# One kernel, one planned order: the delays the planner assumes between engines are changed

## The chip, the core and the metric

The kernel runs on one core of one Trainium2 chip. The metric is the device time of one execution in microseconds (us). Before the change it is 1154.88 us, the median of three runs (1153.9 to 1155.04).

A core has five engines with a queue each, and every queue runs strictly in its own program order: TensorE (PE, matmuls; its weight loads are shown as PEld), VectorE (DVE), ScalarE (ACT), GpSimd (POOL) and SyncE (SP, which here only issues DMAs). Between queues there are semaphores: an instruction that waits holds up everything behind it on its own engine.

## What is computed

One transformer block on 2 x 2048 tokens of width 512: causal attention with 16 query heads of 32 and a single shared key/value head, a layernorm, a mixture of 8 experts (top 2, hidden width 128), a second layernorm.

```python
qkv = einsum('bsd,ed->bse', x, Wqkv_w) + Wqkv_b            # q: 16 heads of 32, one k, one v
scores = where(causal, einsum('bqhd,bkd->bhqk', q, k) / sqrt(32), min)
ctx = einsum('bhqk,bkd->bqhd', softmax(scores), v)
x = layernorm(x + einsum('bsd,ed->bse', ctx, out_w) + out_b)
top, sel = top_k(x @ router_w.T, 2);  gate = softmax(top)
h = silu(xb @ w1[e]) * (xb @ w3[e]);  y = sum over sel of gate * (h @ w2[e])     # bf16
x = layernorm(x + y)
```

## The kernel before

**Tiles and blocks.** The 4096 tokens are 32 tiles T of 128, in 8 groups G of 4. In its batch entry a tile has `own = T % 16` earlier tiles, so it is weighed against `own + 1` key tiles. That makes 272 blocks (tile, key tile) in all, 16 of them in the last tile, T = 31.

**One block.** PE makes the scores of all 16 heads (`three<-qT,kT_g` and one bank, 8 row-tiled matmuls of 64 x 512; lines 1081 to 1095). ACT takes the exponential in two instructions, 1536 elements from `three` and 512 from the bank, into a tile `pT` (for the tile's own diagonal block: `acc`, which POOL then masks). PE weighs the values (`cs<-pT,v_g`, lines 1161 to 1166). DVE adds `pT` to `acc` (`add_up`, line 1204), so that the sums of the softmax need one pass at the end. There is only one `three`, three `pT`, two `acc` and four more PSUM banks (`bank`) that everything else shares.

**Behind the last block of a tile** (`after`): sums by PE with a matrix of ones, a 32 x 32 transposition on DVE (`lT`), reciprocals, `ctxT`, the output projection (`bank<-woT,ctxT`), the residual, then `layernorm`: DVE statistics (`st`, `mv`, `r`), two small POOL instructions on `r`, and ACT or, in the last tile, DVE for `x`.

**Experts** (`experts`, by groups of four tiles; singly in the last group): transposition of x1, the router (`gates`), then for each tile and each half of the experts `up` (w1), `half` (w3), ACT's tanh into `a`, a DVE product, a POOL product with the gates (`a<-a,gt`; in single tiles the gate is applied on DVE instead), a DVE product into `h`, a DMA transposition of `h`, and `down` with the second residual and layernorm.

**What sets the order.** A planner written in the kernel, class `Order` (lines 67 to 236), runs at build time. Every piece of work is a generator that yields `step(engine, us, ...)`: the engine, an assumed duration, the buffers it needs (`acquire`), the marks it needs (`after`), a priority and, for filler work, a due time. The planner keeps a clock for every engine, takes the engine whose next step can start first, of its ready steps the one of lowest `prio`, and emits its instructions there. Each engine's queue is then kept in just this order (`keep_in_program_order`, line 252: all instructions carry L248 in the profile). Scores of attention have `prio` 0, weighings 1, and fillers (projections, output projections, experts) 1.5 or more unless their due time is near, when they go to -0.5.

A step of `us` occupies its engine for `us`. What depends on it can start only `LAT[engine]` later:

```python
self.now, self.end = t, t + us
if s.eng != SP:
    self.busy[s.eng] = self.end
self.end += self.LAT[s.eng]
```

`mark` and `free` record this later time, so LAT is the delay that the planner assumes for a semaphore between engines. On PE a change of the array's tiling costs `TURN` besides. The durations that bear on the change are: scores 0.86 on PE, the exponential 0.25 + 0.44 per bank on ACT (1.57 for `three`), 2.3 on DVE for an addition to `acc`, 2.25 on POOL for `a<-a,gt` and for the mask, 1.95 on POOL for both `r` instructions. Nothing of LAT reaches the chip: there the semaphores decide, and only the order is fixed.

The whole program is also built a second time behind a check of the sums (`run(True)`); that part isn't executed with these inputs.

Of the kernel before, what the change touches and what calls it, by code (L numbers as in the profile page):

```python
# [33 lines left out]
PE, ACT, DVE, POOL, SP = "PE", "ACT", "DVE", "POOL", "SP"  # L34
# [32 lines left out]
class Order:  # L67
# [1 line left out]

    LAT = {PE: 0.3, ACT: 0.15, DVE: 0.15, POOL: 0.15, SP: 0.0}
    LOOK = {DVE: 1.0}
    TURN = {FULL: 0.1, ROW: 0.2, COL: 0.115, TILE: 0.115}
    CAP = 5.0
# [1 line left out]
    def __init__(self, banks, **rings):  # L77
        self.rings = {name: [n, []] for name, n in rings.items()}
        self.banks = [None] * banks
        self.busy = {e: 0.0 for e in self.LAT}  # L80
        self.sig = {}
# [11 lines left out]
    def advance(self, gen, got):  # L93
        end = self.end
        try:
            s = gen.send(got)
        except StopIteration:
            return
        lat = s.lat if s.lat is not None else -self.LAT[PE] if s.open_ else 0.0
        self.count += 1  # L100
# [119 lines left out]
    def issue(self, t, p):  # L220
# [8 lines left out]
# [3 lines that stand above are left out]
        if s.due is not None and s.eng == PE:  # L232
# [1080 lines left out]
```

## Time and profile before

| | us |
|---|---|
| median of the three runs | 1154.88 |
| the profiled execution, device time | 1154.49 |
| its span, first to last instruction | 1152.7 |
| PE busy | 1087.3 (94%) |
| DVE busy | 923.6 (80%) |
| ACT busy | 735.8 (64%) |
| POOL busy | 452.2 (39%) |

The granted TensorE clock was 0.998 over the run. Busy time of matmuls has modelled ends, so PE's 94% says that PE is seldom without work, not that it is at its peak. Each group of instructions has its mean duration: an addition to `acc` on DVE takes 2349 ns, x238; an exponential of `three` 1543 ns; of a bank 682 ns; `a<-a,gt` on POOL 2060 ns, x56; the two `r` instructions on POOL 1572 and 1350 ns. After the first 30 us the DMA engines are busy for 6 to 20% of any longer stretch.

### The profile page before, as it was taken

The numbers are of one execution on the slowest core, as the hardware profiler recorded it, in microseconds if no ns is written. First come the engines' busy times: TensorE is split into PE (matmuls) and PEld (weight loads), VectorE is DVE, ScalarE is ACT, GpSimd is POOL, SyncE is SP. The second block draws the span as 40 slices with busy tenths as digits, with TensorE's granted clock in tenths as the row PEclk, the third lists the DMA queues.
The fourth block names the chain that finished last, engine by engine and source line by source line (L and its number), as shares of the span: only waits on it lengthen the run. The fifth ranks groups of instructions, "written<-read, shape, count | busy, mean of one in ns | idle before, by whom it ended". The sixth has DMA issues, their size and how long they took to land.

```text
span 1152.7 us, 29615 instructions
## 1 busy us (share of the span) xinstructions
PE 1087.3 (94%) x13046; PEld 329.4 (29%) x13046; DVE 923.6 (80%) x1171; ACT 735.8 (64%) x839; POOL 452.2 (39%) x291
## 2 busy tenths in 40 slices
PE   8999999999999999999999999999999899899975
PEld 4322222222322233232222222223233233233222
DVE  2348767878998789989747877779989999999975
ACT  2455667576676677775656556666676667767561
POOL 3212432213451245445325324416556455345110
PEclk9999999999999999999999999999999999999999
DMA  9301001002110021111001000001011011011011
GB/s 253 75 17 56 10 10 48 11 11 56 30 47 1 11 66 29 38 30 38 19 20 56 20 10 19 20 20 38 20 37 40 20 26 42 19 30 48 20 29 31
DMA packets 57404, 40.94 MB, mean 36 GB/s; under 512 B 42729, under 2 KB 43753, under 8 KB 57266
## 3 DMA queue, kind: packets, MB, share of 16 engines
q1 hardware_dynamic: 47248, 34.63, 11.2%
q0 software_dynamic: 9360, 3.15, 2.4%
q8 instruction: 104, 1.70, 0.6%
q10 hardware_dynamic: 658, 1.18, 0.3%
q14 instruction: 34, 0.28, 0.1%
HBM read 25.58 MB, written 8.39 MB: 29 GB/s over the span
## 4 chain that ended last, share of the span: by engine, by line
PE 58%; DVE 28%; issue 5%; POOL 4%; ACT 4%; DMA 0%; DVEq 0%; ACTq 0%; POOLq 0%
PE bank L248 33%; DVE acc L248 15%; PE three L248 14%; PE cs L248 11%; ACT pT L248 2%; POOL r L248 2%; POOL a L248 2%; DVE st L248 2%; DVE x L248 2%; DVE h L248 2%; DVE lT L248 1%; DVE ctxT L248 1%; DVE a L248 1%; DVE fine L248 1%; DVE mx L248 1%
## 5 line engine op out<-in xcount | busy, mean ns | idle before, releaser
L248 DVE TENSOR_TENSOR acc<-acc,pT 128x2048 f32<-128x2048 f32 x238 | 559.1, 2349 | 36.7 <-PE cs L248 22.0
L248 ACT ACTIVATE pT<-three,bias 128x1536 f32<-128x1536 f32 x240 | 370.3, 1543 | 266.9 <-PE bank L248 211.2
L248 PE MATMUL three<-qT,kT_g 32*64 32x512 f32 x3264 | 299.5, 612 | 29.9 <-ACT pT L248 21.4
L248 PE MATMUL bank<-qT,kT_g 32*64 32x512 f32 (+1 forms) x1216 | 304.8, 590 | 0.2 <-ACT qT L248 0.2
L248 PE MATMUL cs<-pT,v_g 128*32 128x512 f32 x1920 | 255.4, 603 | 1.6 <-ACT c_sb L248 0.9
L248 POOL TENSOR_TENSOR r<-r,neg_half 128x1 f32<-128x1 f32 x64 | 100.6, 1572 | 360.1 <-DVE r L248 348.4
L248 POOL TENSOR_TENSOR a<-a,gt 128x512 f32<-128x512 f32 x56 | 115.1, 2060 | 164.2 <-DVE a L248 164.2
L248 ACT ACTIVATE pT<-bank,bias 128x512 f32<-128x512 f32 x240 | 163.6, 682 | 0.0
L248 PE MATMUL bank<-w_sb,x1b 128*32 128x512 bf16 x2048 | 127.3, 380 | 2.5 <-DVE x1b L248 0.7
L248 POOL TENSOR_SCALAR_AFFINE_SELECT acc<-acc 128x2048 f32<-128x2048 f32 x32 | 72.2, 2256 | 140.6 <-ACT acc L248 140.6
L248 PE MATMUL bank<-woT,ctxT 128*32 128x512 f32 x1024 | 119.7, 594 | 3.9 <-DVE ctxT L248 3.6
L248 PE MATMUL bank<-xT,wqT 128*32 128x512 f32 x1024 | 122.4, 594 | 0.0
L248 PEld LDWEIGHTS three<-qT,kT_g 32*64 32x64 f32 x3264 | 60.4, 129 | 194.7 <-ACT pT L248 138.5
L248 PEld LDWEIGHTS cs<-pT,v_g 128*32 128x32 f32 x1920 | 40.6, 108 | 178.0 <-issue 172.7
L248 POOL TENSOR_SCALAR r<-mv,r 128x1 f32<-128x1 f32 x62 | 83.7, 1350 | 6.1
L248 PEld LDWEIGHTS <-x1b 128*32 128x32 bf16 x2048 | 57.5, 97 | 84.4 <-issue 47.5
L248 ACT ACTIVATE acc<-three,bias 128x1536 f32<-128x1536 f32 x32 | 49.4, 1544 | 38.0 <-PE three L248 23.0
L248 PE MATMUL bank<-w_sb,hT 128*32 128x512 bf16 x1024 | 62.4, 379 | 2.5 <-DVE h L248 1.4
L248 ACT ACTIVATE x<-x,r 128x512 f32<-128x512 f32 x62 | 50.5, 818 | 6.5 <-POOL r L248 6.5
L248 PEld LDWEIGHTS bank<-woT,ctxT 128*32 128x32 f32 x1024 | 31.1, 109 | 79.9 <-issue 64.3
L248 DVE STREAM_TRANSPOSE lT<-bank 128x512 f32<-128x512 f32 x32 | 22.9, 715 | 38.4 <-PE bank L248 38.4
L248 DVE TENSOR_TENSOR x<-bank,xr 128x512 f32<-128x512 f32 x32 | 22.0, 688 | 39.1 <-PE bank L248 33.3
(110 smaller groups left out, 962.3 us busy)
## 6 DMA issues: line engine op xcount, KB each, us to landing
xg<-in_L_attn_x_dram SPq DMA_DIRECT2D x32, 256.0 KB, 4.0
xr<-in_L_attn_x_dram SPq DMA_DIRECT2D x32, 256.0 KB, 2.6
out_dram<-x SPq DMA_DIRECT2D x32, 256.0 KB, 2.0
w_sb<-in_L_ffn_w_dram POOLq DMA_DIRECT2D x8, 256.0 KB, 9.1
wq_n<-in_L_attn_Wqkv_w_dram ACTq DMA_DIRECT2D x4, 256.0 KB, 5.9
wo_n<-in_L_attn_out_w_dram SPq DMA_DIRECT2D x1, 1024.0 KB
w_sb<-in_L_ffn_w_dram POOLq DMA_DIRECT2D x1, 1024.0 KB, 15.7
hT<-h SPq DMA_TRANSPOSE x31, 3.1
```

The source lines that it names most:

```text
L248: return lambda *a, **k: self.issue(getattr(self.engine, name)(*a, **k))
```

## The change

Two of five delays in the planner become shorter, one becomes longer:

```diff
-    LAT = {PE: 0.3, ACT: 0.15, DVE: 0.15, POOL: 0.15, SP: 0.0}
+    LAT = {PE: 0.18, ACT: 0.1, DVE: 0.15, POOL: 1.0, SP: 0.0}
```

No instruction's work changes. The listing of both programs' queues shows the same matmuls, exponentials, additions and DMAs, in another order on every engine:

- PE changes the tiling of its array 686 times before and 685 times after; all 272 blocks use `three` and one bank in both.
- Between one block's scores and the next block's, PE gets other work. Before, most often a weighing and two filler steps; after, most often a weighing and one.
- The `up` steps of the groups 0 to 6 begin behind score block 47, 80, 116, 162, 194, 217 and 241 before, and behind 61, 109, 134, 192, 215, 242 and 263 after. Group 6 is in work during blocks 241 to 253 before; after, it falls into the last tile (blocks 257 to 272), with its x1 transposed behind block 258.
- In the last microseconds, before: `down` of tile 30, transposition of `h` of tile 31, `down` of tile 31. After: transposition of `h` of tile 31, `down` of tile 30, `down` of tile 31. The router's `trscT` of tile 30 stands before the output projection of tile 31 in the old order and behind it in the new. On DVE the second half of `h` of tile 30 moves in between the halves of tile 31.

## The prediction

> **What bounds the kernel now.** First the page: engines, then the chain that ended last.
>
> ```profile
> PE 1087.3 (94%) x13046; PEld 329.4 (29%) x13046; DVE 923.6 (80%) x1171; ACT 735.8 (64%) x839; POOL 452.2 (39%) x291
> ...
> PE 58%; DVE 28%; issue 5%; POOL 4%; ACT 4%; DMA 0%; DVEq 0%; ACTq 0%; POOLq 0%
> ```
>
> PE sets the end with DVE's help. Where, the stretches say (us; busy of PE, PEld, DVE, ACT, POOL):
>
> ```profile
> 562.00:623.00 61.00, 60.39 (x612) 17.82 (x596) 32.58 (x49) 33.20 (x41) 21.27 (x18) 1.00 0.10 31
> ...
> 949.00:998.00 49.00, 45.58 (x590) 13.98 (x585) 46.46 (x68) 36.40 (x42) 20.23 (x17) 1.00 0.14 39
> ...
> 1112.00:1153.00 41.00, 25.32 (x315) 10.54 (x315) 24.51 (x75) 10.07 (x17) 3.27 (x6) 0.93 0.10 29
> ```
>
> Early PE is full and DVE half idle; late in a batch entry both are at 93 to 95%; the last 41 us are a chain that fills neither. Third, PE's timeline, one block with two filler steps and two blocks without:
>
> ```profile
> 304.78 0.67 PE L248 MATMUL three<-qT,kT_g 32*64 32x512 f32 x6
> ...
> 305.82 1.06 PE L248 MATMUL cs<-pT,v_g 128*32 128x512 f32 x8
> 306.70 1.91 PE L248 MATMUL bank<-w_sb,hT 128*32 128x512 bf16 x32
> 308.54 0.67 PE L248 MATMUL three<-qT,kT_g 32*64 32x512 f32 x6
> ...
> 344.16 0.68 PE L248 MATMUL three<-qT,kT_g 32*64 32x512 f32 x6 [0.61 <-ACT pT L248]
> ...
> 346.94 0.68 PE L248 MATMUL three<-qT,kT_g 32*64 32x512 f32 x6 [0.67 <-ACT pT L248]
> ...
> 348.13 1.54 ACT L248 ACTIVATE pT<-three,bias 128x1536 f32<-128x1536 f32 x1 [0.67 <-PE bank L248]
> ```
>
> From start to start, scores take 1.04 us, a weighing 0.88, two fillers 1.84: 3.76. With no filler the single `three` sets 2.78: 1.19 until ACT starts (346.94 to 348.13), 1.54 of exponential, 0.05 back to PE. Last, POOL:
>
> ```profile
> 1000.17 2.28 DVE L248 TENSOR_TENSOR acc<-acc,pT 128x2048 f32<-128x2048 f32 x1
> ...
> 1000.33 3.01 POOL L248 TENSOR_TENSOR a<-a,gt 128x512 f32<-128x512 f32 x1 [15.64 <-DVE a L248]
> ...
> 1003.38 0.69 DVE L248 TENSOR_TENSOR h<-bank,a 128x512 bf16<-128x512 f32 x1 [0.93 <-POOL a L248]
> ```
>
> The tile `a` (ns, least, median, most), and the list of waits:
>
> ```profile
> L248 POOL TENSOR_TENSOR a<-a,gt x56: 1029/2954/3157, 243.5 to 1042.7; 128x512 f32<-128x512 f32 x56
> ```
>
> ```profile
> DVE h L248 <- POOL a L248: 16.9, 23, 1.2
> ```
>
> POOL's product takes 2.95 us (median) beside an addition, 1.03 at best, and DVE then stands before `h`: 16.9 us in 23 waits.
>
> **The new delays against the chip.** The old plan thinks the bare loop lasts 0.86 + 0.2 (turn) + 0.3 + 1.57 + 0.15 = 3.08 us; the new, 0.86 + 0.2 + 0.18 + 1.57 + 0.1 = 2.91; the trace has 2.78. Scores, weighing and one filler (0.98 with the turn) make 2.90, so one filler leaves the old plan a hole, into which it starts a second; the new plan stops at one. Gaps of 2.75 to 3 us between scores, by these step prices, grow from 22 to 111 of 271, those of 3.5 to 4 fall from 140 to 38. For POOL the old plan has 2.25 + 0.15 = 2.4 for `a`, the new 3.25 (trace 2.95); for both `r` 2.1 and 2.95 (trace 1.57 + 1.35 = 2.92).
>
> **PE's work: nothing.** I price each PE step by the lower-quartile start-to-start time of its kind and count both listings: 1062.1 us before, 1062.6 after; 686 and 685 turns. The change can only move lost time, 1152.7 - 1062.1 = 90.6: 11.9 until tile 1's first score (at 42.6; priced 30.8), 49.8 until tile 31's (1054.8), 10.1 until the last score (1111.9), 18.7 behind it.
>
> **Until tile 31.** I cut the way to tile 31 into 15 stages, at tiles 1, 4, 7, 9, 11, 13, 15, 17, 20, 22, 24, 26, 28, 29, 30 and 31, and price PE's and DVE's work in each (DVE's by the means of its rows, a tile beginning with its first addition). Before: tiles 9 to 11 PE 78, DVE 75, took 79; 13 to 15 PE 96, DVE 101, took 102; 29 to 30 PE 44, DVE 47, took 50. The larger of the two, stage by stage, is 47, 76, 64, 78, 85, 101, 61, 53, 45, 63, 74, 82, 49, 47, 54, in sum 979; the stretch took 1012, 3.4% more. After: 49, 74, 54, 76, 82, 96, 66, 55, 42, 67, 65, 80, 50, 42, 58, in sum 956: the expert work left for tile 31. 956 x 1.034 = 988.5, from 42.0: tile 31's first score at 1030.5, where before had 1054.8.
>
> **What moves and costs nothing.** ACT's instructions move too; ACT is 64% busy and needs 1.54 + 0.69 of each 2.90, and what it delays is in the 3.4%. The mask on POOL (2.02 median) is now planned at 3.25; in both orders 31 of 32 tiles' own weighings stand over 6 us of PE work behind their scores, against 1.19 + 1.54 + 0.69 + 2.02 = 5.4 needed: other blocks' work covers it. On SP, group 6's stores and `h` transpositions move into the last tile past the `xr` loads (2.0, 3.1 and 2.6 us to land): `xr` is wanted 10 us later, and DMA is 10% busy there; without that cover a store costs 2 us once.
>
> **POOL.** The DVE work queued between `a` and its `h` is POOL's cover. Before, 11 of 56 lie at 2.3 and 19 below 2.8; after 8 below 2.8, most at 3 to 5.7. What is missing to 3.2 sums to 20.9 before (measured wait 16.9) and 17.8 after; but six of the new ones are nearly uncovered (0 to 1.4), where no addition runs beside POOL: at 1.3 each instead of 3.2, 6.5 remains. A saving of 3 to 10; I take 5, as some waits lie where PE is the longer. 1025.5. If no wait is on the path, 0.
> The GPSIMD Engine Reference of the Trainium skill (Specifications) says that GpSimd shares its SBUF interfaces with VectorE and contends with two-input VectorE instructions. By that POOL's cost is a stretch, no constant delay, and the 1.0 is wrong wherever DVE isn't adding; by the rule the saving nears 10, by a constant 2.95 it is 3.
>
> **Tile 31 until `lT`.** Before, its own block is weighed 11.2 us behind its first score; after, PE has 13.9 in between, + 0.9 lost as before: 1040.3. From there to the DVE transposition `lT` the old trace takes 53.2 (1066.1 to 1119.28) for 48.1 of priced DVE work, of which the bare `three` loop costs some 3.4 more than in the new order; without it 49.8, a factor of 1.035. New: DVE 68.5, PE 63.4. 68.5 x 1.035 = 70.9: `lT` at 1111.2. Bounds 68.5 and 68.5 x 1.106 = 75.8.
>
> **From `lT`.** Before 33.4 us. `lT` to the end of the output projection: + 0.4, as DVE's `x1b` is on the way. Then the router of tile 30 starts behind the projection: by the durations in the trace the two halves of `h` of tile 31 end 15.4 us behind the projection where before it was 13.4, and tile 30's second half at 13.6. `down` of tile 30 stands ahead of tile 31's in PE's queue and needs a DMA transposition (3.1 us to landing, median): it starts at some 17.1, tile 31's at 19.0, before 14.7. + 4.3. Queued behind that are the residual, layernorm and the last store, the end itself. Bounds: + 2 (the 13.4 to 15.4 alone) and + 6 (landing 1.7 later). 33.4 + 0.4 + 4.3 = 38.1.
>
> **Sum.** 1111.2 + 38.1 = 1149.3 of span. The median stands 2.2 above the profiled span (1154.88 - 1152.7): **1151.5 us**, 0.3% faster. Startup: its four transpositions change places, + 0 to 0.5, hidden by the first loads.
>
> **Rivals.** *The last tile eats more than the rest gains* (slower). Place: tile 31 between its own weighing and `lT`. Group 6's eight halves and four layernorms now run there, each a chain PE, ACT, DVE, POOL, DVE through two `a`; the old last 41 us show what chains do (DVE 24.5 of 41). If the stretch takes 82 instead of 70.9 (factor 1.2 on DVE): 1162.6. It decides from 76.6 on, where the total passes 1157.2. Against: 14 additions are there to fill DVE. *No change*: POOL's waits lie where PE is longer, nothing is saved: 1156.5, and with a stage factor of 1.033 1155.5. *Much faster*: with honest delays the stages lose 2% (tiles 9 to 11 lost 1.4, 1 to 4 2.6): 956 x 1.02, 13.4 less: 1138.1. For it: ACT and POOL are modelled closely now; against: in a 2.90 rhythm DVE (2.35 of it an addition) has no slack for `a` and `h`. That the order stays the same is excluded by the listing.
>
> **How the numbers follow.** Forecast (own range 1144 to 1152.5) 0.37, much faster 0.12, no change 0.16, slower 0.35. What can be told from no change is 0.2%, 2.3 us: faster 0.49, same 0.16, slower 0.35. Range: the stage factor between 1.026 and 1.042 is 8 us either way; POOL 3.5 or 5; `lT` + 5; tail + 2: 1139 to 1167.
>
> **What would show it.** Right: first score of tile 31 about 25 to 30 us earlier than 1054.8; DVE's wait for POOL `a` below 12; PE's last `down` behind a DMA transposition; from `lT` to the end about 38. Wrong: more PE waits for ACT or DVE in the 2.9 rhythm (a stage factor above 1.04), or `lT` more than 76 behind the own weighing.

## The result and the profile after

| | before | after |
|---|---|---|
| median of the runs on one chip, us | 1154.45 (4 runs) | 1168.94 (4 runs, 1167.58 to 1172.56) |
| ratio, 95% interval | | 1.013 [1.0105, 1.0155] |
| profiled execution, us | 1154.49 | 1172.56 |
| its span, us | 1152.7 | 1170.7 |
| first score of tile 31 at | 1054.8 | 1035.5 |
| last score at | 1111.9 | 1124.3 |
| from the last score to the end | 40.8 | 46.4 |

The change makes the kernel 1.3% slower. The profiled execution is the slowest of the four; its sums are made against its own 1170.7 us. The page of the changed kernel, engines and the chain that ended last:

```profile
PE 1095.9 (94%) x13046; PEld 330.9 (28%) x13046; DVE 928.8 (79%) x1171; ACT 736.8 (63%) x839; POOL 432.5 (37%) x291
...
PE 62%; DVE 25%; issue 6%; ACT 5%; DMA 1%; POOL 1%; DVEq 0%; ACTq 0%; POOLq 0%; SPq 0%
```

The shares hardly move, so the page alone does not say where 18 us went. The stretches do (us; busy time of PE, PEld, DVE, ACT, POOL; granted clock, DMA share, GB/s): tiles 1 to 30, the start of tile 31, two stretches of its blocks, and what is behind the last score.

```profile
42.00:1035.00 993.00, 951.34 (x11326) 271.50 (x11329) 814.29 (x913) 669.24 (x747) 377.01 (x234) 1.00 0.10 28
1035.00:1052.00 17.00, 15.94 (x225) 6.31 (x221) 13.14 (x19) 11.01 (x15) 10.86 (x11) 1.00 0.13 33
1052.00:1080.00 28.00, 23.83 (x288) 6.33 (x280) 24.96 (x44) 15.85 (x18) 11.49 (x7) 0.94 0.10 30
1080.00:1124.00 44.00, 38.80 (x567) 16.54 (x562) 35.96 (x65) 21.20 (x28) 20.46 (x15) 1.00 0.15 38
1124.00:1170.70 46.70, 29.77 (x395) 14.14 (x387) 28.90 (x102) 11.62 (x20) 3.57 (x8) 0.92 0.18 48
```

Until tile 31 PE is busy for 96% of the time. In tile 31 it is 85% at 1052 to 1080, where DVE is at 89%. In the old order PE was at 84% behind tile 31's own weighing as well (38.49 of the 46 us from 1066 to 1112), but without group 6's work; the change brings that work here, and it does not fill PE. What happens in it is on PE's timeline (two transpositions of group 6's x1, the own block's weighing, a later weighing, then scores of three blocks):

```profile
1040.94 0.66 PE L248 MATMUL bank<-ident,x 128*128 128x128 f32 x4 [0.86 <-DVE h L248]
1041.80 0.66 PE L248 MATMUL bank<-ident,x 128*128 128x128 f32 x4 [0.20 <-ACT pT L248]
...
1050.68 1.07 PE L248 MATMUL cs<-acc,v_g 128*32 128x512 f32 x8
...
1060.17 1.63 PE L248 MATMUL cs<-pT,v_g 128*32 128x512 f32 x8 [0.72 <-ACT pT L248]
1061.73 0.67 PE L248 MATMUL three<-qT,kT_g 32*64 32x512 f32 x6
...
1064.57 0.68 PE L248 MATMUL three<-qT,kT_g 32*64 32x512 f32 x6 [1.73 <-ACT pT L248]
...
1073.73 0.85 PE L248 MATMUL three<-qT,kT_g 32*64 32x512 f32 x6 [1.72 <-ACT pT L248]
...
1074.31 1.13 PE L248 MATMUL three<-qT,kT_g 32*64 32x512 f32 x6
```

Between the scores at 1061.73 and 1064.57 PE has no other work and waits 1.73 us for the exponential that frees `three`; the same at 1073.73. At the first there are no fillers, because group 6's gates are only now being made. At the second the gates are ready, but the two halves begun since then still hold both tiles `a`, and PE's next `up` comes only at 1077.10:

```profile
1064.94 0.19 DVE L248 TENSOR_TENSOR gt<-gt 128x32 f32<-128x32 f32 x1
...
1070.41 4.01 POOL L248 TENSOR_TENSOR a<-a,gt 128x512 f32<-128x512 f32 x2 [6.73 <-DVE a L248]
```

With the shorter waits above (0.86, 0.20 and 0.72 us) PE stands idle for 5.2 us. The last line of PE's timeline is a matmul that takes 1.13 us where its like takes 0.62: the clock is at half there (last section).

The list of waits (in all, times, longest), first a line of before, then two of the change:

```profile
DVE acc L248 <- PE cs L248: 22.0, 11, 9.1
```

```profile
DVE acc L248 <- PE cs L248: 44.1, 13, 13.8
...
DVE h L248 <- POOL a L248: 5.8, 7, 1.4
```

DVE's wait for POOL's product fell from 16.9 to 5.8 us, as the longer delay would have it (but it is down to 10.4 in `d1_pe_act` below, without that delay); its additions' wait for weighings doubled, from 22.0 to 44.1. That second wait is not what costs the time in tile 31: `t3_due` below has the same 44.1 and is 7.0 us faster than `t1_new_tail` with 44.0. Last, the tail's timeline:

```profile
1151.88 0.38 PE L248 MATMUL bank<-ident_b,h 128*128 128x128 bf16 x4 [1.47 <-DVE h L248]
...
1152.94 1.24 SPq L1014 DMA_TRANSPOSE hT<-h  x1
...
1153.97 1.00 PE L248 MATMUL bank<-ident_b,h 128*128 128x128 bf16 x4 [1.70 <-DVE h L248]
...
1156.04 5.30 PE L248 MATMUL bank<-w_sb,hT 128*32 128x512 bf16 x64 [1.06 <-DMA hT<-h]
```

The last matmuls of `down` stand behind tile 30's DMA transposition, issued at 1152.94: PE's program has `down` of tile 30 ahead of tile 31's, and behind the transposition of tile 31's `h`. PE waits 1.47 and 1.70 us for the halves of that `h` and another 1.06 us for the DMA. The 64 matmuls of both `down` then take 5.30 us: the granted clock is 0.50 from 1156.0 to 1159.4.

### The profile page after: what moved, and what is told of

Same layout as the page of the kernel before. It is cut to its first block, busy times and chain, and to the rows that moved or that the text cites. A ratio compares the mean times of both kernels' runs of the same rounds, so it can differ in the third digit from the quotient of the medians.

```text
span 1170.7 us, 29575 instructions
## 1 busy us (share of the span) xinstructions
PE 1095.9 (94%) x13046; PEld 330.9 (28%) x13046; DVE 928.8 (79%) x1171; ACT 736.8 (63%) x839; POOL 432.5 (37%) x291
## 4 chain that ended last, share of the span: by engine, by line
PE 62%; DVE 25%; issue 6%; ACT 5%; DMA 1%; POOL 1%; DVEq 0%; ACTq 0%; POOLq 0%; SPq 0%
PE bank L248 32%; PE three L248 16%; PE cs L248 14%; DVE acc L248 13%; ACT pT L248 3%; DVE h L248 2%; DVE x L248 1%; DVE a L248 1%; DVE st L248 1%; DVE lT L248 1%; DVE ctxT L248 1%; ACT acc L248 1%; DVE mx L248 1%; DVE fine L248 1%; POOL a L248 1%
## 5 line engine op out<-in xcount | busy, mean ns | idle before, releaser
L248 DVE TENSOR_TENSOR acc<-acc,pT 128x2048 f32<-128x2048 f32 x238 | 568.9, 2390 | 59.9 <-PE cs L248 44.1
L248 POOL TENSOR_TENSOR r<-r,neg_half 128x1 f32<-128x1 f32 x64 | 90.4, 1412 | 380.2 <-DVE r L248 351.4
L248 POOL TENSOR_TENSOR a<-a,gt 128x512 f32<-128x512 f32 x56 | 105.2, 1884 | 138.3 <-DVE a L248 137.7
L248 POOL TENSOR_SCALAR_AFFINE_SELECT acc<-acc 128x2048 f32<-128x2048 f32 x32 | 80.0, 2501 | 186.5 <-ACT acc L248 186.4
L248 PEld LDWEIGHTS cs<-pT,v_g 128*32 128x32 f32 x1920 | 43.5, 108 | 164.3 <-issue 153.8
L248 PEld LDWEIGHTS <-x1b 128*32 128x32 bf16 x2048 | 56.2, 97 | 97.3 <-issue 60.4
L248 POOL TENSOR_SCALAR r<-mv,r 128x1 f32<-128x1 f32 x62 | 72.1, 1162 | 6.1
L248 PE MATMUL bank<-w_sb,hT 128*32 128x512 bf16 x1024 | 65.0, 387 | 2.4 <-DVE h L248 1.4
L248 ACT ACTIVATE a<-bank 128x512 f32<-128x512 f32 x64 | 38.4, 600 | 33.0 <-PE bank L248 24.2
L248 DVE SCALAR_TENSOR_TENSOR a<-a,bank 128x512 f32<-128x512 f32 x64 | 43.4, 680 | 16.1 <-ACT a L248 16.0
L248 ACT ACTIVATE x<-x,r 128x512 f32<-128x512 f32 x62 | 50.5, 816 | 7.2 <-POOL r L248 7.2
```

The lines of the kernel that those rows point to most:

```text
L248: return lambda *a, **k: self.issue(getattr(self.engine, name)(*a, **k))
```

## The experiments

All are timed against the kernel before on the same chip, in three sets (before: 1154.54, 1154.37 and 1154.16). Where a table gives "stall", it is the time at which a score starts less the priced PE work ahead of it, by the prices of the prediction; "tail" is the time from the last score to the end. Both are read from the one profiled execution of each kernel. The change and `t1_new_tail` have the same PE order until behind block 271 and still differ in stall by 1.3 us until tile 31 and by 2.8 in it; up to 1.7 of each is a spell of half clock (last section) that only the change's execution has. The times are medians; executions of one kernel lie up to 5 us apart (`d1_pe_act` 1153.79 to 1158.63).

### First set: the parts of the change, and the theory that group 6 comes too late

`d1_pe_act` has the two shorter delays only, `d2_pool` the longer one only. `CAP` is the factor of the planner's due times: with 2.0 in place of 5.0 a group of experts becomes urgent earlier. `d3_new_cap2` is the changed kernel with it, `d4_old_cap2` the kernel before with it.

```diff
 # d1_pe_act
-    LAT = {PE: 0.18, ACT: 0.1, DVE: 0.15, POOL: 1.0, SP: 0.0}
+    LAT = {PE: 0.18, ACT: 0.1, DVE: 0.15, POOL: 0.15, SP: 0.0}
 # d2_pool
+    LAT = {PE: 0.3, ACT: 0.15, DVE: 0.15, POOL: 1.0, SP: 0.0}
 # d3_new_cap2 (changed kernel) and d4_old_cap2 (kernel before)
-    CAP = 5.0
+    CAP = 2.0
```

> Only the two shorter delays (PE 0.18, ACT 0.1; POOL stays 0.15). In the listing this order has group 6's up steps behind blocks 261 to 269 and 116 gaps of 2.75 to 3 us, nearly as the changed kernel (263 to 270, 111). Theory A (experts that come late and crowd the last tile cost the time): 1163 to 1171 us. Theory B (the dense 2.9 us rhythm of the blocks costs the time, wherever the experts are): the same, 1163 to 1171. Theory C (the longer POOL delay costs the time): 1152 to 1157, as before.

> Only the longer POOL delay (1.0; PE 0.3 and ACT 0.15 as before). The listing keeps group 6 at blocks 239 to 251 and 26 close gaps. Theories A and B: 1149 to 1156 us, as before or a little less, since DVE's wait for POOL's product (16.9 us before, 5.8 in the changed kernel) falls below 10. Theory C: 1163 to 1171.

> The changed kernel with the planner's CAP at 2.0 instead of 5.0: filler work becomes urgent earlier. The listing brings group 6's up steps to blocks 242 to 249 and DVE's priced work between the last tile's own weighing and lT from 69.8 to 32.3 us, while 108 of the close gaps stay. Theory A: 1150 to 1160 us, and own weighing to lT falls from about 80 us to 35 to 42. Theory B: 1163 to 1170, since the rhythm stays. Theory C: 1163 to 1170.

> The kernel before with CAP 2.0: group 6 at blocks 232 to 242, 28 close gaps. A control for the run above. Theory A: some of the old last tile's crowding goes too, 1146 to 1154 us. Theory B: 1152 to 1157, nothing gained. If CAP itself costs (fillers forced between scores), over 1157 in both runs.

| | us | ratio to before | group 6 `up` at blocks | tail, us |
|---|---|---|---|---|
| before | 1154.54 | | 241 to 253 | 40.8 |
| the change | 1168.94 | 1.013 [1.0105, 1.0155] | 263 to 270 | 46.4 |
| d1_pe_act | 1156.85 | 1.0018 [1.0006, 1.003] | 261 to 269 | 45.9 |
| d2_pool | 1154.53 | 1.0004 [0.9995, 1.0014] | 239 to 251 | 40.1 |
| d3_new_cap2 | 1172.84 | 1.0164 [1.0147, 1.0181] | 242 to 249 | 39.9 |
| d4_old_cap2 | 1183.08 | 1.0247 [1.023, 1.0264] | 232 to 242 | 41.7 |

Three simple theories fall. The shorter delays alone cost 2.3 us, the longer one alone nothing; only together do they cost 14. Group 6 in the last tile is not by itself the loss, as `d1_pe_act` has it there too. And bringing all groups forward costs more than it gains: in `d3_new_cap2` the stall until tile 31 is 76.6 against 69.5. In the old order the same `CAP` costs 28.5 us (`d4_old_cap2`), so these two runs don't tell what an earlier group 6 alone would bring.

### Second set: the tail, and the size of POOL's delay

`t1_new_tail` is the changed kernel, `t2_pe_act_tail` is `d1_pe_act`, both with the router of single tiles (the small transposition `trscT` in `gates`) put ahead of other PE work. The order of PE's steps stays as it was until behind block 271.

```diff
 # gates(), t1_new_tail and t2_pe_act_tail
-                (m,) = yield step(PE, 0.12, ["m"], array=FULL, due=due)
+                (m,) = yield step(PE, 0.12, ["m"], array=FULL, due=due, prio=-2.5 if n == 1 else None)
 # q1_pool050 and q2_pool090 (changed kernel)
-    LAT = {PE: 0.18, ACT: 0.1, DVE: 0.15, POOL: 1.0, SP: 0.0}
+    LAT = {PE: 0.18, ACT: 0.1, DVE: 0.15, POOL: 0.5, SP: 0.0}
+    LAT = {PE: 0.18, ACT: 0.1, DVE: 0.15, POOL: 0.9, SP: 0.0}
```

> The changed kernel with one priority more: the router's transposition trscT of single tiles goes first. The listing is the same on PE up to behind block 271 (step 1143 of 1183); after that trscT of tile 30 stands before the output projection, and down of tile 30 before the transposition of h of tile 31, as in the kernel before. Tail theory (down of tile 30 waits for its DMA transposition ahead of tile 31's): last score to end falls from 46.4 to about 41, total from 1168.9 to 1163 to 1165.5 us. If the tail's length has another cause: 1167 to 1170.

> The same priority in the kernel with only the two shorter delays (PE 0.18, ACT 0.1), which has the same long tail (45.9 us, 3.8 us of wait at down of tile 30) and took 1156.9 us. Tail theory: 1151.5 to 1153.5 us, so faster than the kernel before (1154.5). Otherwise 1156 to 1158.

> PE 0.18, ACT 0.1 and POOL 0.5, half way to the change. Theory D (a longer POOL delay costs more the longer it is, once PE and ACT are short): between 1158 and 1164 us. Theory E (no trend: every setting of the delays is another order, and orders of the same make lie a per cent apart by where they happen to leave PE without a ready step): anywhere from 1152 to 1170, and not between its neighbours. It has the long tail as well.

> PE 0.18, ACT 0.1 and POOL 0.9, close to the change (1.0), but another order from block 2 on, with the short tail. Theory D: 1161 to 1165 us (the changed kernel's 1168.9 less some 5 of tail). Theory E: it may as well be 1152 to 1158.

| | us | ratio to before | stall until tile 31 | lost in tile 31 until the last score | tail |
|---|---|---|---|---|---|
| the change | 1168.94 | 1.013 [1.0105, 1.0155] | 69.5 | 16.9 | 46.4 |
| t1_new_tail | 1164.49 | 1.0092 [1.0076, 1.0108] | 68.2 | 14.1 | 39.3 |
| t2_pe_act_tail | 1151.5 | 0.9982 [0.9972, 0.9991] | 62.4 | 9.1 | 40.6 |
| q1_pool050 | 1155.84 | 1.0012 [1.0003, 1.0022] | 61.4 | 8.6 | 46.6 |
| q2_pool090 | 1169.75 | 1.0138 [1.0122, 1.0154] | 69.0 | 17.3 | 41.8 |

The order behind block 271 is settled as the cause of the long tail: the edit gives 4.4 us to the changed kernel and 5.3 to the other. In the timeline of `t1_new_tail`, `down` of tile 30 runs first and waits for no DMA, and tile 31's `h` is transposed and used behind it.

```profile
1148.30 1.91 PE L248 MATMUL bank<-w_sb,hT 128*32 128x512 bf16 x32 [1.37 <-DVE h L248]
1150.14 0.62 PE L248 MATMUL bank<-ident_b,h 128*128 128x128 bf16 x8
1151.87 1.91 PE L248 MATMUL bank<-w_sb,hT 128*32 128x512 bf16 x32 [1.10 <-ACT hT L248]
```

The wait for the DMA is only a part of it. The two `down` take 1.91 us each here; in the profiled executions with the transposition of tile 31's `h` ahead of them (the change, `d1_pe_act`, `q1_pool050`, `m_maskr`) their 64 matmuls took 5.30, 6.04, 5.33 and 6.48 us, in part at half clock. No run separates the wait from the clock. The tails themselves differ by 7.1 us, more than the 4.4: in `t1_new_tail` some of the PE work that the change has behind the last score stands ahead of it.

The size of POOL's delay does not act gradually: 0.15 and 0.5 are alike (1156.9, 1155.8, both with the long tail), 0.9 and 1.0 are alike (1169.8, with a short tail, and 1168.9, with a long one); the theory of a gradual cost missed both its times (1158 to 1164 and 1161 to 1165). Something flips between 0.5 and 0.9, and it costs in two places: 5 to 8 us until tile 31, and 5 to 9 in it.

### Third set: what flips

Two runs split POOL's delay by the kind of step. `m_a` assumes 1.0 us behind the product `a<-a,gt` only, `m_maskr` behind the masks and `r` only. `t3_due` adds one line to `t1_new_tail`: group 6's experts are due when tile 31 begins. `q3_tail` is `q1_pool050` with the tail's edit.

```diff
 # m_a and m_maskr (changed kernel, LAT of POOL 0.15)
-        self.end += self.LAT[s.eng]
+        self.end += 1.0 if s.eng == POOL and s.us == 2.25 and s.prio is None else self.LAT[s.eng]
+        self.end += 1.0 if s.eng == POOL and s.prio in (-1.0, -2.0) else self.LAT[s.eng]
 # t3_due (t1_new_tail)
-                    experts(G, [t] if alone else list(range(TG)), start_of((G + n_x1) * TG)),
+                    experts(G, [t] if alone else list(range(TG)), start_of(seq[-1] if G == NGRP - 2 else (G + n_x1) * TG)),
```

> The changed kernel with the delay of 1.0 us assumed behind one kind of POOL step only, the product of `a` with the gates; behind the masks, the `r` of layernorm and all other POOL steps 0.15 as before. The order: group 6's `up` at blocks 261 to 268 (the change 263 to 270), x1 of group 6 is taken up at 1036 of the plan as in the change (0.15 everywhere: 1027), group 5 runs until block 256. Theory 'product': what costs in the change is the long delay behind `a`, which holds `a`, a bank and `h` longer in the plan, stretches every group of experts, brings group 5 to its end two blocks later and so lets group 6's route begin inside tile 31: time 1160 to 1171, stall until tile 31's first score 67 to 70, 14 or more lost in tile 31 until the last score. Rival 'mask and layernorm': the long delay behind the masks and `r` costs: here 1153 to 1158, stall 61 to 64. Rival 'scatter': any new order can fall on either side, and the value of the delay says nothing: then this run and the next one need not differ, or differ the other way.

> The complement of the run before: 1.0 us assumed behind the masks and the `r` of layernorm, 0.15 behind the product of `a`. Group 6's `up` at blocks 261 to 269, as with 0.15 everywhere. Theory 'product': 1153 to 1158, stall until tile 31's first score 61 to 64, some 9 lost in tile 31 until the last score. Rival 'mask and layernorm': 1160 to 1171. Rival 'scatter': no relation.

> The changed kernel with the router of single tiles ahead (as in t1_new_tail, 1164.5) and one more line: group 6's experts become due when tile 31 begins. PE's order is that of t1_new_tail until block 256; then group 6's four transpositions of x1 and its gates come one to two blocks earlier, and its `up` at blocks 261 to 268 in place of 263 to 270. Theory 'late gates of group 6': the bare scores at blocks 261 to 265 cost the change some 5 of the 6 to 8 us that it loses in tile 31 more than the order with POOL at 0.15: time 1157 to 1160.5, lost in tile 31 until the last score 7 to 10. Rival: the loss follows from how `a`, DVE and PE meet along the whole tile, wherever group 6 begins: 1162.5 to 1167, still 13 or more lost in tile 31.

> PE 0.18, ACT 0.1, POOL 0.5 (as q1_pool050, 1155.8) with the router of single tiles ahead, as in t2_pe_act_tail. Expected by the tail theory: last score to the end 40 to 41 in place of 46.6, so 1150 to 1152, below the kernel before by some 0.3%. If the short tail in t2_pe_act_tail was luck of its order: 1154 to 1157.

| | us | ratio to before | stall until tile 31 | lost in tile 31 until the last score | tail |
|---|---|---|---|---|---|
| m_a | 1165.85 | 1.0097 [1.008, 1.0114] | 67.3 | 18.5 | 40.4 |
| m_maskr | 1160.99 | 1.0067 [1.0052, 1.0083] | 66.6 | 7.6 | 46.2 |
| t3_due | 1157.52 | 1.0035 [1.0022, 1.0048] | 66.6 | 8.0 | 39.6 |
| q3_tail | 1152.11 | 0.9981 [0.9972, 0.999] | 60.4 | 8.0 | 44.3 |

**The tail again.** `q3_tail` came at 1152.11 where 1150 to 1152 was expected, but its tail is 44.3 and not 40 to 41. Its `down` waits for no DMA and runs at 1.91 us twice; PE waits 1.99 us for DVE's `h` ahead of it. Why this tail is longer than the others was not tried.

**Tile 31.** One line that brings group 6's route forward takes 7.0 us off `t1_new_tail`, at the top of what was expected, and the loss in tile 31 falls from 14.1 to 8.0. The 24 us behind tile 31's own weighing, first of the changed kernel, then of `t3_due` (same columns as above):

```profile
1051.75:1075.75 24.00, 19.83 (x236) 5.25 (x240) 22.81 (x41) 13.34 (x16) 11.36 (x6) 0.97 0.06 24
```

```profile
1048.38:1072.38 24.00, 23.28 (x329) 7.99 (x324) 23.32 (x29) 15.86 (x19) 15.76 (x8) 1.00 0.15 45
```

PE is busy for 19.83 us in the one and 23.28 in the other, at a granted clock of 0.97 and 1.00. The timeline of `t3_due` in that stretch, own weighing and scores:

```profile
1047.34 1.04 PE L248 MATMUL cs<-acc,v_g 128*32 128x512 f32 x8
...
1058.10 0.67 PE L248 MATMUL three<-qT,kT_g 32*64 32x512 f32 x6
...
1060.93 0.68 PE L248 MATMUL three<-qT,kT_g 32*64 32x512 f32 x6 [0.72 <-ACT pT L248]
...
1064.70 0.67 PE L248 MATMUL three<-qT,kT_g 32*64 32x512 f32 x6
```

A wait of 0.72 us is left there, where the change has two of 1.7. `t1_new_tail`, which differs by the one line alone, has all five waits of the change (0.86, 0.20, 0.72, 1.73 and 1.72 us): 4.5 of the 6.1 us. So what costs is not that group 6 runs in the last tile, but that some steps of tile 31 stand with nothing between them until its chain is going.

**The flip is mostly behind the product.** With the long delay behind `a` alone (`m_a`), tile 31 loses 18.5 us as in the change; with it behind masks and `r` alone (`m_maskr`), 7.6 as without it. Against `t2_pe_act_tail`, which has a short tail too, `m_a` is 14.4 us slower, and `t1_new_tail` with both delays 13.0. Spells of half clock are in the losses of tile 31: one in the change and in `t2_pe_act_tail`, two in `m_a`, one of double length in `q2_pool090`, none in the others. At 1.7 us for each 3.4 (an estimate), 14 to 15 remain in the change, `t1_new_tail`, `m_a` and `q2_pool090`, and 7 to 9 in the other orders of the last two tables.

In the plan of the change and of `m_a` group 6's route could begin only at 1036 of plan time, with a delay of 0.15 at 1027. That this is because in the plan group 5's products hold `a` and a bank longer is the theory; no run tries this step by itself. In `m_a` the bare scores are these:

```profile
1063.25 0.68 PE L248 MATMUL three<-qT,kT_g 32*64 32x512 f32 x6 [1.71 <-DVE a L248]
...
1066.14 0.68 PE L248 MATMUL three<-qT,kT_g 32*64 32x512 f32 x6 [1.77 <-ACT pT L248]
```

The gates are done at 1058.1 there and the `up` steps begin behind block 261, as in `t3_due`; PE waits for DVE's product on `a`, which stands behind two additions. And only a part of `m_a`'s loss lies here: PE is busy for 16.08 of the 20 us from 1051 to 1071, and for 14.27 of the 18 us from 1097 to 1115. So `m_a` has the change's loss in size, but in part at other places.

**The stages before are only half settled.** From tile 1's first score to tile 31's, the stall grows by 50.5 us in `t2_pe_act_tail`, 49.0 in `q3_tail` and 49.8 before; by 53.9 in `m_a`, 56.1 in `m_maskr`, 54.5 in `t3_due` and 56.1 in the change, whose spell at 439.2 us is in it. Either kind of long delay costs 3 to 6 there, and both together no more than one: the expectation that `m_maskr` would be at 1153 to 1158 was missed (1160.99, in the range of its rival 'mask and layernorm', 1160 to 1171). It is 4.1 above `d1_pe_act`; in the profiled executions tile 31 begins 3.8 us later (1037.6 against 1033.8), and 1.5 less is lost in it. The losses lie spread, 2 us at tiles 4 to 7 and some 2 at tiles 17 to 20 in most of these orders. Which step makes them was not tried.

**The best version.** `t2_pe_act_tail` (1151.5) and `q3_tail` (1152.11) are alike and beat both kernels, the one before by 0.2% (ratios 0.9982 and 0.9981): PE 0.18, ACT 0.1, POOL 0.15 or 0.5, and the router of single tiles ahead.

### The sum

The runs make a ladder from the best version to the change: 1151.5 (`t2_pe_act_tail`), + 6.0, most of it in the stages (`t3_due`, 1157.52; stall until tile 31 66.6 against 62.4), + 7.0 for group 6's late start in tile 31 (`t1_new_tail`, 1164.49), + 4.4 for the tail: 1168.94. The shorter delays of PE and ACT with a mended tail are 2.9 us faster than the kernel before (1151.5 against 1154.37); the tail's edit on the old delays, whose tail is 40.8 as it is, was not tried. `t3_due` and `t2_pe_act_tail` differ in all of POOL's delay and in group 6's due time, so the 6.0 is a difference of two orders and no single mechanism.

## Why the prediction was wrong

It said 1151.5 us, in a range of 1139 to 1167, with 0.49 on faster. The time is 1168.94.

*Right: PE's work.* PE has the same matmuls, and the priced work of both orders was 1062.1 and 1062.6; all of the 18 us of span are lost time.

*Right in number: the stage factor.* 956 x 1.034 = 988.5 was forecast between the first scores of tiles 1 and 31. It took 1035.5 - 43.5 = 992.0, and 1.7 of that are a spell of half clock at 439.2 us (another, at 39.9, is the 1.5 by which tile 1 begins late). But another order does better: `q3_tail` took 1030.7 - 41.5 = 989.2 with 4 us more of priced PE work done by then (its block 257 stands behind 970 us of priced work, the change's behind 966). A factor carried over from the old order cannot tell one new order from another. Tile 31's first score came 19.3 us earlier than before (1035.5 against 1054.8), where 25 to 30 was named as a sign of being right.

*Wrong: "POOL. A saving of 3 to 10; I take 5."* The wait fell by 16.9 - 5.8 = 11.1, more than said, and saved nothing. DVE's additions became longer by nearly as much, as the groups show, before and after (busy in all and mean ns):

```profile
L248 DVE TENSOR_TENSOR acc<-acc,pT 128x2048 f32<-128x2048 f32 x238 | 559.1, 2349 | 36.7 <-PE cs L248 22.0 <-ACT pT L248 8.2 <-ACT xT L248 0.2
```

```profile
L248 DVE TENSOR_TENSOR acc<-acc,pT 128x2048 f32<-128x2048 f32 x238 | 568.9, 2390 | 59.9 <-PE cs L248 44.1 <-ACT pT L248 5.1 <-DVE acc L248 1.4
```

Additions and waits for POOL together are 559.1 + 16.9 = 576.0 before and 568.9 + 5.8 = 574.7 after; in `d1_pe_act` 564.9 + 10.4 = 575.3, in `q3_tail` 568.2 + 6.7 = 574.9. In these orders DVE either waits for POOL, or adds beside it and is slowed by it. But the total doesn't decide alone: in `d2_pool` it is 557.7 + 8.3 = 566.0, 10 us less, and the time is as before (1154.53). The prediction had noted this conflict as a stretch and no constant delay, and still booked the wait as a gain.

*Wrong, and the largest: "Tile 31 until `lT`: 68.5 x 1.035 = 70.9".* From the own weighing's end (1050.68 + 1.07) to `lT` it took 80.3:

```profile
1132.07 0.71 DVE L248 STREAM_TRANSPOSE lT<-bank 128x512 f32<-128x512 f32 x1
```

The bounds were 68.5 and 75.8. This is the rival "the last tile eats more than the rest gains", with its place (tile 31 between its own weighing and `lT`) and nearly its size (82); it was to decide from 76.6 on, and did. The step failed by taking DVE's work as the bound, by taking 3.4 us off the old stretch for bare scores that the new order was thought to be without, and by giving PE the old order's small losses. Of the 9.4 that are missing, 4.2 are PE's three waits behind the own weighing (0.72, 1.73, 1.72) and up to 1.7 the spell of half clock behind them; the rest is not assigned. What the listing already showed was that group 6's gates stand behind block 258 and its first `up` behind 263, with scores of blocks 262 and 264 that no filler follows: a hole can be counted on the listing, and was not. With the gates one to two blocks earlier the same stretch takes 1120.47 - 1048.38 = 72.1 in `t3_due`, near the forecast, and 77.8 in `t1_new_tail`, which differs by that line alone.

*Off by 1.4: the own weighing.* 13.9 + 0.9 behind tile 31's first score was forecast; it was 16.2, with two waits (0.86 and 0.20 us) at the transpositions of group 6's x1.

*Right in the order, in number partly by luck: the tail.* From `lT` to the end 38.1 was forecast, 1170.7 - 1132.1 = 38.6 measured; the DMA transposition of tile 30's `h` is where it was said to be. But `down` began 16.1 us behind the output projection where 17.1 was forecast, and its 64 matmuls took 5.30 us instead of twice 1.91, in part at half clock, which the forecast hadn't. The loss was taken as given, and `t1_new_tail` shows that one priority takes most of it away (34.9 from `lT` to the end).

In sum, against 1149.3 of span: tile 1 begins 1.5 later (43.5 against 42.0), the stages take 3.5 more, POOL saves no 5, own weighing 1.4, tile 31 9.4 (1.7 of it a spell of half clock at 1074.1), tail 0.5: 21.3 of the 21.4 that are missing.

## What to carry to other kernels

A planner's delay should be what the trace shows for that place. POOL's 1.0 us was right only where DVE adds beside it: the product takes 2.95 us in the median before and 1.04 after, when the order has moved it elsewhere (1.04 in `d1_pe_act` too, where POOL's delay is as before). When an order is generated, price it by the listing near the end of the program as carefully as the mean rhythm: look for stretches in which the bound engine's steps stand with no filler between them, and ask what makes the fillers late. A wait that shrinks is no gain if the engine's total (work and wait) stays, and, as `d2_pool` shows, a total that shrinks need not be one either.

## What was not expected of the hardware

*Half clock without a long idle time.* The granted TensorE clock falls to 0.50 for single windows of 3.4 us in the middle of the program. Stretches of the changed kernel ahead of, within and behind one such window, and the other one that lies ahead of tile 31:

```profile
1070.50:1073.70 3.20, 1.52 (x24) 0.23 (x16) 2.87 (x3) 1.56 (x2) 3.20 (x2) 1.00 0.00 0
1074.10:1077.50 3.40, 3.40 (x28) 0.54 (x16) 2.94 (x3) 2.11 (x3) 0.32 (x1) 0.50 0.02 5
1077.50:1080.50 3.00, 3.00 (x52) 1.04 (x48) 1.46 (x2) 0.86 (x3) 0.63 (x1) 1.00 0.46 87
439.20:442.60 3.40, 3.40 (x28) 0.59 (x16) 2.23 (x9) 2.23 (x4) 1.06 (x1) 0.50 0.02 5
```

In the 3.2 us ahead PE was busy for 1.52 only (28 matmuls then run at half clock for 3.4 us), and its longest gap there was 1.72 us. The Trainium skill's page "TensorE: Matmul & The Clock Gate", Part 1, has the half clock come behind at least one idle window of about 3.4 us; its section on a second failure mode (PSUM-queue depth-cycling) tells of another kernel in which frequent short idling brings it, and these rows agree with that one. A bare score loop can thus be charged twice. Each window costs up to 1.7 us where PE is the bound (an estimate: half of 3.4). In the profiled executions the kernel before has none until its tail, the change three ahead of it (39.9, 439.2, 1074.1) and two in it, the first on `down`.

*A steady sum on DVE.* That additions and waits for POOL come to 575 us in so many orders (574.7 to 576.0 in before, the change, `d1_pe_act`, `q1_pool050`, `q3_tail`, `m_maskr` and `t3_due`; 571.5 in `m_a`, 571.0 in `q2_pool090` and 566.0 in `d2_pool`) was not looked for; in the two runs with `CAP` 2.0 it is 572.1 (`d3_new_cap2`) and 579.6 (`d4_old_cap2`).
